# One-hot graph sums on TensorE: four summing matmuls behind each batch of picks, or one after each picked bucket

## The chip, the cores and the metric

The kernel runs on one core of a Trainium2 chip. The metric is device time in microseconds for one execution of the whole program. Three runs of the kernel before are shown, and their median is what a change is measured against. Traces are of one further execution, taken by the hardware profiler. Engines are called as the profile calls them: PE is the matrix engine's matmul, PEld its weight load, DVE the vector engine, ACT the scalar engine, POOL the general one, and SP the one that issues most transfers.

## The reference, cut to what matters

The graph has 6250 nodes with 128 features and 206250 directed edges (100000 drawn pairs in both directions, and a loop at each node). After a layer norm, an encoder and a ReLU, two message layers run, then three averaging layers. The part that the change touches is the message layer:

```python
m = jnp.concatenate([h[row], h[col]], axis=-1)
m = jax.nn.relu(m @ msg_W1[l].T + msg_b1[l])
m = m @ msg_W2[l].T + msg_b2[l]
agg = jax.ops.segment_sum(m, col, num_segments=h.shape[0])
upd = jnp.concatenate([h, agg], axis=-1) @ upd_W[l].T + upd_b[l]
h = _layer_norm(h + upd, ln_g[l], ln_b[l])
```

The first product splits in two: a row of A (source node) plus a row of B (target node) for each edge, then a ReLU. W2 is applied after the sum, since a sum of products is the product of the sum.

## The kernel before, in words

The nodes are cut into 49 blocks of 128. For each target block `w` the edges that end in it are sorted into buckets of up to 128 edges, one bucket for each source block and a 50th for what did not fit. The 50 buckets form 13 batches: twelve of four buckets and a last one of two (`batches`, index `i`). A step is one batch of one target block, and there are 49 x 13 = 637 steps in each of the two message layers (`l`).

**Picks.** `picked` (L556) gets the edges' rows A + B by multiplying with one-hot matrices. Each bucket takes six bfloat16 matmuls of 128x128: three with the source one-hots as weights (L565; A stands in three bfloat16 parts, for accuracy) and three with the target one-hots (L567). So a full step has 24 picks, all into one PSUM bank `pe`, of which there are three. ACT then applies the ReLU into a tile `m` (L574 or L577).

**Sums.** `summed` (L580) adds the rows of a bucket into the target nodes. Its weights are again one-hots, but as 4-byte numbers (`hd`), made by ACT in `widened` (L516). There are two kinds, chosen by `parts`. In the first layer's batches 0, 3, 6, 9 and 12, and in all of the second layer, `m` holds two parts: ACT writes a rounded one (L574), DVE writes what the rounding left (L554, in `refine`), and one float32r matmul of 256 or 258 columns per bucket sums both. In the other batches of the first layer `m` is plain float32 with 129 columns, and each sum shows as two matmul instructions in the trace. These two kinds have the tile names `hd_r` and `hd` in the profile. All sums of a target block go into one PSUM bank `agg`.

**Order.** The code writes one step after the other. A step fetches a later batch's data, makes the one-hots of the batch two ahead (`hot_at`: L88 and L491 on DVE), refines the batch before (`refine`, L554), picks its own batch, widens its own one-hots, and then settles: `settle(2)` sums the batch of two steps ago, since two batches may stay pending. In the second layer four counting matmuls follow (`counts`, L524). Last come single stages of work that lags or leads: the update of the block before (`behind`), the target rows of the next (`other`), and the sort of a later block's edges (`ahead`, first layer only). When the last batch of a block has been summed, `settle` starts that block's update (L590, a copy of `agg` by ACT).

PE executes in the order in which its instructions stand. The framework orders each engine's instructions by the order of the code and by its own plan of when things are ready. On PE the trace has the order that the code writes, while on ACT the casts of L516 run well before the code's place.

Of the kernel before, what the change touches and what calls it, by code (L numbers as in the profile page):

```python
# [67 lines left out]
def fast(tc, dram, ident, miss_i, x, src, dst, weights, columns, rows, out, edges):  # L68
# [12 lines left out]
    with ExitStack() as ctx:  # L81
# [9 lines left out]
        def bank(name="mm"):  # L91
            return psum.tile([B, 512], F32, name=name, bufs={"pe": 3, "so": 1}.get(name, 2))
# [151 lines left out]
        def nodes(w):  # L244
            return slice(w * B, (w + 1) * B)
# [229 lines left out]
        def fetch(l, w, i):  # L475
            cols = batches[i]
            n, c0 = len(cols), cols[0]
            v = both.tile([B, 8, B], BF16, name="v_all", bufs=4)
            nc.sync.dma_start(v[:, :2 * n], svd[w:w + 1, 2 * c0:2 * (c0 + n), :].to_broadcast([B, 2 * n, B]))
            h = None  # L480
            if l == 1:
                h = late.tile([B, 2, B, 2], BF16, name="hd_b", bufs=6)
                nc.sync.dma_start(h[:, :n // 2].rearrange("p r v e -> p (r v e)"), ohd[w, :, c0 * B:(c0 + n) * B])
            spread[l, w, i] = v, h
# [9 lines left out]
        def hot_first(w, i):  # L494

            cols = batches[i]
            n, c0 = len(cols), cols[0]
            hot = early.tile([B, 2, B, 2], BF16, name="hot", bufs=5)
            one_hots(hot[:, :n // 2], sv[w][:, c0:c0 + n])
            t, _ = node_hot(0, w, i)  # L500
            stores.append((ohd[w, :, c0 * B:(c0 + n) * B], hot[:, :n // 2].rearrange("p r v e -> p (r v e)")))
            return t, hot, None

        def hot_again(w, i):

            cols = batches[i]
            n, c0 = len(cols), cols[0]
            t, h = node_hot(1, w, i)
            hs = late.tile([B, 2, B, 2], BF16, name="hs", bufs=4)
            one_hots(hs[:, :n // 2], sources[:, w, c0:c0 + n])  # L510
            return t, h, hs

        def widened(l, i, hot, n):
            hd = (late if l else early).tile([B, 4, B], F32R if parts(l, i) else F32, name="hd_r" if parts(l, i) else "hd",
                                                   bufs=4 if l else 2 if parts(l, i) else 3)
            nc.scalar.copy(hd[:, :n].rearrange("p (r e) v -> p r e v", e=2), hot[:, :n // 2].rearrange("p r v e -> p r e v"))  # L516
            return hd
# [22 lines left out]
        def counted(w, kept):  # L540
            c2 = late.tile([B, B], U8, name="c2")
            nc.vector.tensor_add(c2, kept[0], kept[1])
            stores.append((cnt[w, :, w, :], c2))

        def parts(l, i):

            return l == 1 or i % 3 == 0
# [3 lines left out]
        def refine():  # L551
            while rough:
                m, pe, n = rough.pop(0)
                nc.vector.scalar_tensor_tensor(m[:, :n, :D], pe, 0.0, m[:, :n, D:2 * D].bitcast(F32), op0=OP.max, op1=OP.subtract)  # L554

        def picked(w, l, i, t, b3):  # L556

            cols = batches[i]
            n = len(cols)
            pe = bank("pe")  # L560
            for j, c in enumerate(cols):
                o = slice(j * D, (j + 1) * D)
                block = w if c == NB else c
                for k in range(3):
                    nc.tensor.matmul(pe[:, o], t[:, j, 0, :], a3[l][:, block, k, :], start=(k == 0), stop=False)  # L565
                for k in range(3):
                    nc.tensor.matmul(pe[:, o], t[:, j, 1, :], b3[:, k, :], start=False, stop=(k == 2))  # L567
            pe = pe[:, :n * D].rearrange("p (j f) -> p j f", f=D)
            k = int(parts(l, i))
            ring = rings[k] if l == 0 else late_ring  # L570
            m = ring[turn[k] % len(ring)]
            turn[k] += 1
            if k:
                nc.scalar.activation(m[:, :n, D:2 * D], pe, AF.Relu)  # L574
                rough.append((m, pe, n))
            else:
                nc.scalar.activation(m[:, :n, :D], pe, AF.Relu)  # L577
            return m

        def summed(l, i, m, hd, agg):  # L580

            two = parts(l, i)
            to = agg[:, :2 * D + 2 * (1 - l)] if two else agg[:, D:2 * D + 1]
            for j, c in enumerate(batches[i]):
                nc.tensor.matmul(to, hd[:, j, :], m[:, j, :to.shape[1]], start=(c == 0), stop=(c == NB))  # L585

        def update(w, l, agg):
            xw = xws.pop(w, None)
# [43 lines left out]
        def settle(most):  # L632

            nonlocal behind
            while len(pending) > most:
                w, l, i, m, hd, agg = pending.pop(0)
                if not agg:
                    agg.append(bank("agg"))
                summed(l, i, m, hd, agg[0])
                if i == NI - 1:  # L640
                    for _ in behind:
                        pass
                    behind = update(w, l, agg[0])
                    next(behind)
# [8 lines left out]
        for l in range(2):  # L653
            if l == 1:
                refine()
                settle(0)
                while stores:
                    nc.sync.dma_start(*stores.pop(0))
                part_of.close()
                right.close()  # L660
                h2[0] = ctx.enter_context(tc.tile_pool(name="h2_0", bufs=1, side="right")).tile(
                    [B, NB, 2, D], F32R, name="h2_0")
                late = part_of.enter_context(tc.tile_pool(name="late", bufs=2))
                late_ring = rings[1] + [late.tile([B, 4, 2 * D + 2], F32R, name=f"m2{k}", bufs=1) for k in (2, 3)]
            def fetch_at(q):
                if q < NB * NI:
                    fetch(l, q // NI, q % NI)

            def hot_at(q):
                w, i = divmod(q, NI)  # L670
                if w >= NB:
                    return None
                return hot_again(w, i) if l else hot_first(w, i)

            A = 2
            for q in range(A + 2):
                fetch_at(q)
            hots = [hot_at(q) for q in range(A)]
            kept = []
            for w in range(NB):  # L680
                agg, kept, kept_before = [], [], kept
                b3, b3_next, other = b3_next[0], [], iter(())
                for i, cols in enumerate(batches):
                    q = w * NI + i
                    fetch_at(q + A + 2)
                    while stores:
                        nc.sync.dma_start(*stores.pop(0))
                    hots.append(hot_at(q + A))
                    refine()
                    t, target, source = hots.pop(0)  # L690
                    m = picked(w, l, i, t, b3)
                    hd = widened(l, i, target, len(cols))
                    pending.append((w, l, i, m, hd, agg))
                    settle(2)
                    if l == 1:
                        counts(w, i, source, target, kept)
                        if i == 0 and w:
                            counted(w - 1, kept_before)
                    if i > 1:
                        next(behind, None)  # L700
                        if l == 1:
                            next(behind, None)
                    if i == 4 and (l, w) != (1, NB - 1):
                        other = target_rows((w + 1) % NB, l + (w + 1) // NB, b3_next)
                    next(other, None)

                    for _ in range(2 if steps < q + 2 * NI - 1 and (q < 6 or i % 3 == 0) else 1):
                        next(ahead, None)
                        steps += 1
                    assert i != 6 or l or w + 1 == NB or w + 1 in sv  # L710
                    if l == 1 and i == 6:
                        xws[w] = work.tile([B, D], F32, name="xw")
                        nc.sync.dma_start(xws[w], x[nodes(w), :])
        refine()
        settle(0)
        counted(NB - 1, kept)
        while stores:
            nc.sync.dma_start(*stores.pop(0))
# [296 lines left out]
```

## Time and profile before

| what | value |
|---|---|
| median of three runs | 3890.51 us (3890.47 to 3892.3) |
| the profiled execution's own time | 3893.41 us |
| its span, first to last instruction | 3891.6 us |
| mean granted TensorE clock | 0.996 |
| first message layer, sums on PE | from 102.9 to 1559.8 us |
| second message layer, sums on PE | to 2943.8 us |
| averaging layers | the rest |
| busy in 100 to 1558 us: PE, DVE, ACT | 1452.70, 1364.05, 857.59 us |
| busy in 1558 to 2945 us: PE, DVE, ACT | 1382.28, 1092.70, 1118.35 us |

A line of the timeline has the start in microseconds, the time from the start of the first to the end of the last instruction of the group, the engine, the line of the code, the operation, the tiles written and read, the shapes, and how many instructions are merged. Matmuls overlap one another, so the shown duration of one (219 ns for a pick) is its latency. What a matmul costs PE is the distance from its start to the next one's start.

### The profile page before, as it was taken

The page shows a single profiled execution, that of the slowest core. Times are in us where ns is not written, and L with a number is a line of the kernel's source. Part 1 is how long each engine was busy: PE and PEld are TensorE (multiplying, and loading weights), DVE is VectorE, ACT ScalarE, POOL GpSimd, SP SyncE. Part 2 cuts the span into 40 slices and gives each one's busy share as a digit, 9 for nine tenths or more (in the row PEclk, how much of TensorE's full clock was granted, in tenths as well). Part 3 has the DMA queues.
Part 4 walks back from the last instruction along what each step waited for, and adds up shares of the span by engine and source line. Part 5 has one row for each costly group of instructions (what it writes and reads, how often), then busy time and mean ns, then how long its engine had stood idle before and what let it go on. Part 6 is the DMA issues. An engine that isn't in the chain of part 4 may idle for free. (4 is left out here: it accounts for less than half of the span.)

```text
span 3891.6 us, 117300 instructions
## 1 busy us (share of the span) xinstructions
PE 3820.3 (98%) x45975; PEld 3578.7 (92%) x45975; DVE 2924.2 (75%) x7365; ACT 2531.0 (65%) x4850; POOL 35.1 (1%) x29
## 2 busy tenths in 40 slices
PE   5999999999999999999999999999999999999998
PEld 3999999999999999999999999999998888888887
DVE  7999999999999997787778787877874444444443
ACT  5555555555555555788888888888885555555554
POOL 3000000000000000000000000000000000000000
PEclk8999999999999999999999999999999999999999
DMA  3555555555555555777777777777774444444554
GB/s 107 160 173 167 168 171 175 165 168 172 175 165 168 174 167 169 201 213 211 210 204 214 206 213 212 211 211 206 211 209 136 132 128 114 132 128 114 159 155 124
DMA packets 656079, 671.11 MB, mean 172 GB/s; under 512 B 113200, under 2 KB 504474, under 8 KB 655386
## 3 DMA queue, kind: packets, MB, share of 16 engines
q1 hardware_dynamic: 650124, 662.26, 58.5%
q8 instruction: 362, 5.93, 0.6%
q14 instruction: 203, 1.66, 0.2%
q10 hardware_dynamic: 5390, 1.26, 0.1%
HBM read 534.28 MB, written 128.99 MB: 170 GB/s over the span
## 5 line engine op out<-in xcount | busy, mean ns | idle before, releaser
L565 PE MATMUL pe<-a,ot 128*128 128x128 bf16 x14700 | 1622.0, 219 | 0.0
L567 PE MATMUL pe<-b,ot 128*128 128x128 bf16 x14700 | 1620.7, 219 | 0.0
L565 PEld LDWEIGHTS <-ot 128*128 128x128 bf16 x14700 | 1044.0, 98 | 17.0
L567 PEld LDWEIGHTS <-ot 128*128 128x128 bf16 x14700 | 1026.4, 98 | 0.0
L778 PE MATMUL pe<-cf,h 128*128 128x512 f32 (+1 forms) x3822 | 924.3, 394 | 2.2 <-DVE cf L770 1.1
L778 PEld LDWEIGHTS pe<-cf,h 128*128 128x128 f32 x3822 | 677.3, 190 | 141.9 <-ACT cf L770 1.2
L574 ACT ACTIVATE m<-pe 128x512 fp32r<-128x512 f32 (+1 forms) x882 | 508.2, 576 | 327.3 <-PE pe L567 324.7
L491 DVE TENSOR_SCALAR ot<-v_all,part 128x1024 bf16<-128x1024 bf16 (+1 forms) x1274 | 599.2, 470 | 105.7 <-PE pe L567 87.5
L770 ACT CAST cf<-c 128x2048 fp32r<-128x2048 uint8 (+2 forms) x253 | 433.8, 1714 | 338.7 <-PE pe L778 283.5
L554 DVE SCALAR_TENSOR_TENSOR m<-pe,m 128x512 fp32r<-128x512 f32 (+1 forms) x882 | 579.1, 657 | 56.5 <-ACT m L574 31.0
L585 PE MATMUL agg<-m,hd_r 128*128 128x256 f32 (+1 forms) x3332 | 612.2, 303 | 3.1 <-DVE m L554 3.0
L770 DVE CAST cf<-c 128x2048 fp32r<-128x2048 uint8 (+2 forms) x254 | 280.7, 1105 | 359.0 <-PE pe L778 204.1
L585 PEld LDWEIGHTS agg<-m,hd_r 128*128 128x128 f32 x3332 | 453.9, 190 | 4.0 <-DVE m L554 3.8
L585 PE MATMUL agg<-m,hd 128*128 128x129 f32 x3136 | 435.3, 281 | 0.0
L516 ACT CAST hd_r<-hd_b 128x512 fp32r<-128x512 bf16 (+1 forms) x637 | 384.5, 604 | 8.5 <-DMA hd_b<-ohd 2.6
L585 PEld LDWEIGHTS agg<-m,hd 128*128 128x128 f32 x3136 | 381.0, 191 | 0.0
L516 ACT CAST hd<-hot 128x512 f32<-128x512 bf16 x392 | 242.3, 618 | 194.0 <-DVE hot L88 91.4
L526 ACT CAST ca<-so 128x512 uint8<-128x512 f32 (+1 forms) x637 | 360.2, 565 | 0.4 <-PE so L524 0.4
L577 ACT ACTIVATE m<-pe 128x512 f32<-128x512 f32 x392 | 233.5, 596 | 134.9 <-PE pe L567 133.2
L88 DVE TENSOR_TENSOR hot<-sv,iota 128x512 bf16<-128x512 f16 (+1 forms) x637 | 254.8, 406 | 20.3 <-ACT hd L516 12.0
L88 DVE TENSOR_TENSOR hs<-sources,iota 128x512 bf16<-128x512 f16 (+1 forms) x637 | 258.2, 406 | 5.5 <-PE so L524 1.8
L524 PE MATMUL so<-hd_b,hs 128*128 128x128 bf16 x2450 | 252.2, 222 | 2.3 <-DMA hd_b<-ohd 2.0
(163 smaller groups left out, 3165.2 us busy)
## 6 DMA issues: line engine op xcount, KB each, us to landing
v_all<-svd SPq DMA_DIRECT2D x1176, 256.0 KB, 3.9
c<-cnt SPq DMA_DIRECT2D x216, 512.0 KB, 3.8
ohd<-hot SPq DMA_DIRECT2D x588, 128.0 KB, 3.5
hd_b<-ohd SPq DMA_DIRECT2D x588, 128.0 KB, 3.8
cnt<-ca SPq DMA_DIRECT2D x540, 64.0 KB, 3.6
v_all<-svd SPq DMA_DIRECT2D x98, 128.0 KB, 3.4
xw<-in_x SPq DMA_DIRECT2D x49, 64.0 KB, 3.5
ohd<-hot SPq DMA_DIRECT2D x49, 64.0 KB, 2.2
```

The costliest lines, as they stand in the source:

```text
L88: nc.vector.tensor_tensor(to, v.rearrange("p (r e) -> p r e", e=2).unsqueeze(2).to_broadcast([B, n, B, 2]), iota_2.unsqueeze(1).to_broadca ...
L491: nc.vector.tensor_scalar(t[:, :n].rearrange("p j k s -> p (j k) s"), v[:, :2 * n], part, None, op0=OP.is_equal)
L516: nc.scalar.copy(hd[:, :n].rearrange("p (r e) v -> p r e v", e=2), hot[:, :n // 2].rearrange("p r v e -> p r e v"))
L524: nc.tensor.matmul(pa[:, j * B:(j + 1) * B], source[:, j // 2, :, j % 2], target[:, j // 2, :, j % 2], start=True, stop=True)
L526: nc.scalar.copy(ca[:, :n], pa[:, :n * B].rearrange("p (j d) -> p j d", d=B))
L554: nc.vector.scalar_tensor_tensor(m[:, :n, :D], pe, 0.0, m[:, :n, D:2 * D].bitcast(F32), op0=OP.max, op1=OP.subtract)
L565: nc.tensor.matmul(pe[:, o], t[:, j, 0, :], a3[l][:, block, k, :], start=(k == 0), stop=False)
L567: nc.tensor.matmul(pe[:, o], t[:, j, 1, :], b3[:, k, :], start=False, stop=(k == 2))
L574: nc.scalar.activation(m[:, :n, D:2 * D], pe, AF.Relu)
L585: nc.tensor.matmul(to, hd[:, j, :], m[:, j, :to.shape[1]], start=(c == 0), stop=(c == NB))
L770: (nc.scalar.copy if turn % 2 else nc.vector.tensor_copy)(cf[:, :k, :n].rearrange("p s w d -> p w s d"), c8[:, :n, s % R:s % R + k])
L778: nc.tensor.matmul(p[:, :n * B], h2[l % 2][:, s, k, :], cf[:, s % K, :n].rearrange("p w d -> p (w d)"), start=(s == 0 and k == 0), stop=(s ...
```

## The change

`summed` and `settle` become generators that yield after every sum. `picked` takes such a generator and calls it once after each bucket's six picks. What is left of it is run through behind the picks, before `widened`. Since the pending list now loses its oldest entry before the new one is appended, `settle(2)` becomes `settle(1)`, and the batch summed in a step is the same as before. In a step of four buckets with four sums, PE's order goes from 24 picks and four sums to four times six picks and one sum. A batch of two buckets, each block's last, changes this at its two ends: during its own picks the four sums of batch 10 stand as one sum, six picks, three sums, and its own two sums stand after the first and the second of four buckets.

```diff
-        def picked(w, l, i, t, b3):
+        def picked(w, l, i, t, b3, sums):
...
                 for k in range(3):
                     nc.tensor.matmul(pe[:, o], t[:, j, 1, :], b3[:, k, :], start=False, stop=(k == 2))
+                next(sums, None)
...
             for j, c in enumerate(batches[i]):
                 nc.tensor.matmul(to, hd[:, j, :], m[:, j, :to.shape[1]], start=(c == 0), stop=(c == NB))
+                yield
...
                 if not agg:
                     agg.append(bank("agg"))
-                summed(l, i, m, hd, agg[0])
+                yield from summed(l, i, m, hd, agg[0])
...
                     refine()
                     t, target, source = hots.pop(0)
-                    m = picked(w, l, i, t, b3)
+                    sums = settle(1)
+                    m = picked(w, l, i, t, b3, sums)
+                    for _ in sums:
+                        pass
                     hd = widened(l, i, target, len(cols))
                     pending.append((w, l, i, m, hd, agg))
-                    settle(2)
```

At the end of each layer `settle(0)` is run through in a loop, with the same effect as before.

More of the change, by code (lines that the diff above doesn't have):

```diff
@@ L655, in fast @@
                 refine()
-                settle(0)
+                for _ in settle(0):
+                    pass
                 while stores:
@@ L690, in fast @@
                     t, target, source = hots.pop(0)
-                    m = picked(w, l, i, t, b3)
+                    sums = settle(1)
+                    m = picked(w, l, i, t, b3, sums)
+                    for _ in sums:
+                        pass
                     hd = widened(l, i, target, len(cols))
                     pending.append((w, l, i, m, hd, agg))
-                    settle(2)
                     if l == 1:
@@ L714, in fast @@
         refine()
-        settle(0)
+        for _ in settle(0):
+            pass
         counted(NB - 1, kept)
```

## The prediction

> **What bounds the kernel now.** I read the page's busy times first, then the groups of the sums, then who waits in the two message layers, then single steps in the timeline.
>
> ```profile
> PE 3820.3 (98%) x45975; PEld 3578.7 (92%) x45975; DVE 2924.2 (75%) x7365; ACT 2531.0 (65%) x4850; POOL 35.1 (1%) x29
> L585 PE MATMUL agg<-m,hd_r 128*128 128x256 f32 (+1 forms) x3332 | 612.2, 303 | 3.1 <-DVE m L554 3.0
> L585 PE MATMUL agg<-m,hd 128*128 128x129 f32 x3136 | 435.3, 281 | 0.0
> ```
>
> PE is busy throughout, and busy PE alone proves little, but the last column says that it hardly ever waits ahead of a sum: 3.1 us in 6468 matmuls. Ahead of the picks of L565 and L567 the page has 0.0. PE's order and pitch therefore set the time of both message layers, and there is no idle time on PE that a better order could win back. What remains is what a sum costs by its place. One step each with four and with two sums of the hd_r kind, and one with four of the hd kind (eight matmuls):
>
> ```profile
> 1002.47 0.33 PE L567 MATMUL pe<-b,ot 128*128 128x128 bf16 x3
> 1002.61 0.73 PE L585 MATMUL agg<-m,hd_r 128*128 128x258 f32 x4
> 1003.18 0.34 PE L565 MATMUL pe<-a,ot 128*128 128x128 bf16 x3
> 1003.36 0.33 PE L567 MATMUL pe<-b,ot 128*128 128x128 bf16 x3
> ```
>
> ```profile
> 1000.81 0.33 PE L567 MATMUL pe<-b,ot 128*128 128x128 bf16 x3
> 1000.95 0.49 PE L585 MATMUL agg<-m,hd_r 128*128 128x258 f32 x2
> 1001.28 0.34 PE L565 MATMUL pe<-a,ot 128*128 128x128 bf16 x3
> 1001.46 0.33 PE L567 MATMUL pe<-b,ot 128*128 128x128 bf16 x3
> ```
>
> ```profile
> 1011.65 0.33 PE L567 MATMUL pe<-b,ot 128*128 128x128 bf16 x3
> 1011.82 1.11 PE L585 MATMUL agg<-m,hd 128*128 128x129 f32 x8
> 1012.77 0.33 PE L565 MATMUL pe<-a,ot 128*128 128x128 bf16 x3
> 1012.94 0.33 PE L567 MATMUL pe<-b,ot 128*128 128x128 bf16 x3
> ```
>
> Picks alone come at 0.056 us from start to start (in the rows that follow the first view, 18 of them from 1003.36 to 1004.36), 0.336 a bucket. From the first line to the last of each fence stand six picks and the sums. That leaves 0.89 - 0.336 = 0.554 us for four hd_r sums and 0.65 - 0.336 = 0.314 for two. Two equations: each sum costs 0.120, and a group of sums costs 0.074 on top, whatever its length. The eight hd matmuls leave 1.29 - 0.336 = 0.954.
>
> **Where the fixed cost comes from.** The weight loads around the four sums:
>
> ```profile
> 1002.41 0.21 PEld L567 LDWEIGHTS <-ot 128*128 128x128 bf16 x3
> 1002.58 0.55 PEld L585 LDWEIGHTS agg<-m,hd_r 128*128 128x128 f32 x4
> 1003.17 0.17 PEld L565 LDWEIGHTS <-ot 128*128 128x128 bf16 x3
> ```
>
> Picks' loads follow at 0.056 and the sum's load takes its turn after them (0.17 after the first of three), one matmul ahead at most. Four 4-byte loads span 0.55 where one lasts 190 ns, so they follow at 0.12: in a row each load lies under a sum of about the same length, while the first of a group lies under a 0.056 pick. The pick after the group loads at 1003.17, 0.01 ahead of its matmul and not under the last sum. Both ends are paid once a group.
>
> For the hd kind the same float32 matmul stands in two places, in a row behind others and alone between bfloat16 matmuls:
>
> ```profile
> 1008.37 0.39 PE L254 MATMUL mm<-wt,hT 128*128 128x128 f32 x2
> 1008.59 0.33 PE L565 MATMUL pe<-a,ot 128*128 128x128 bf16 x3
> ```
>
> ```profile
> 2024.21 0.43 PE L254 MATMUL mm<-wt,hT 128*128 128x128 f32 x2
> 2024.49 0.33 PE L565 MATMUL pe<-a,ot 128*128 128x128 bf16 x3
> ```
>
> A pair costs 0.22 to the next pick in the row and 0.28 alone: 0.06 of fixed cost. From the eight: four pairs at 0.22 to 0.225 are 0.88 to 0.90, so 0.954 leaves 0.05 to 0.07. I take 0.055.
>
> **The change, part by part.** It adds and removes no matmul, no DVE or ACT work and no transfer; SP's and POOL's queues keep their order, since fetch and stores stand ahead of the picks as before. What changes is the number of groups.
>
> Extra groups in one target block: first layer, hd_r: batches 0, 3, 6 and 9 go from one group to four (+12), batch 12 from one to two (+1), 13 in all. First layer, hd: batches 1, 2, 4, 5, 7, 8 and 11 +3 each, batch 10, summed in the two-bucket step, +1: 22. Second layer: eleven batches +3, batch 10 +1, batch 12 +1: 35. With 49 blocks: 637 + 1715 = 2352 hd_r groups and 1078 hd groups.
>
> Cost: 2352 x 0.074 = 174.0 us, and 1078 x 0.055 = 59.3 us. All of it is on the path, because PE is what everything waits for. Bounds: the hd_r row at its nearest other is the 0.05 of the hd kind, which makes both kinds 3430 x 0.05 = 171.5; from above 0.08 and 0.065 (the rounding of the rows) make 258. I take 233, since 0.074 is of the same operation in the same place.
>
> The Trainium skill, "TensorE: Matmul & The Clock Gate", speaks against a loss in its section on what each phase is for: the queue pulls weight loads ahead of running matmuls, so that the next weights load while this one multiplies. Taken without limit, that hides every load and the sum is 0, 3890 us. The load rows above show the pull reaching one matmul ahead of a sum, and no further; by them the sum is 233. The same page's section on LDWEIGHTS gives 107 ns for 128 columns as an estimate, which less one pick leaves 51 ns a group and 175 us in all; the row's 0.074 holds the exit as well.
>
> **A wait that comes earlier.** The sums of a batch need DVE's refinement (L554). The first now stands one bucket into the step, three buckets (1.0 us) earlier. Behind it on PE are all later picks, and ACT's ReLU waits for those. In the first layer, at the start of a block:
>
> ```profile
> 1029.69 0.42 DVE L554 SCALAR_TENSOR_TENSOR m<-pe,m 128x256 fp32r<-128x256 f32 x1
> ```
>
> ```profile
> 1030.70 0.48 PE L585 MATMUL agg<-m,hd_r 128*128 128x258 f32 x2
> ```
>
> The refinement ends at 1030.11. That step's picks start at 1029.39, so its first sum would stand at 1029.73, 0.38 too early. In the next step the refinement ends at 1031.62 and the first sum would stand at 1031.37, 0.25 too early. That is 0.63 x 49 = 31 us if DVE stands where it stood. But a block gets 13 x 0.074 + 22 x 0.055 = 2.2 us longer on PE, with DVE's work unchanged, so DVE comes earlier by more than it lacks. I take 0, and 31 as the end. In the second layer DVE waits 42 times, 102.9 us in all, for the transfer of xw (L619). After one such wait the refinement ends at 2038.60, and the sums at 2039.27 would stand 1.0 earlier, at 2038.26: 0.34 too early, 42 x 0.34 = 14 us at most. Transfers don't get slower, steps get longer: I take 7. A gain is excluded here, since PE has only those 3 us to win. DVE's waits for picks (L491, 87.5 us) move with PE and cost nothing, being DVE's idle time.
>
> **Sum.** 174 + 59 + 7 = 240 us. Against the profiled execution's own 3893.4 us this is 4133; that execution stands 2.9 us above the median of the runs, so against the median 3890.5 + 240 = 4130.
>
> **Rivals.**
> - *A lone group is cheaper* (0.05 for both kinds, no stall): 171.5, so 4062. For it: the hd kind shows 0.05 to 0.06. Against it: four and two hd_r sums agree on 0.074.
> - *Refinement stalls PE* as often as today's places say: 233 + 31 + 14 = 278, so 4169. For it: DVE is 94% busy in the first layer (1364 of 1458 us). Against it: the longer block.
> - *The loads hide after all* (the other side). If a sum's load could start two matmuls ahead, entry and exit vanish; an hd_r sum would cost what its columns take, under 0.115 (256 columns at 0.056 for 128 are 0.112), and the 2450 hd_r sums would gain at least 0.008 each, 20 us, and today's 882 groups their 0.074, 65 us: 3805. It decides as soon as a lone sum costs less than the present mean of 0.554 / 4 = 0.139. Against it: the load of 1002.58.
> - *The order stays*: the framework's plan sets each engine's order, on ACT it moves casts (L516) ahead. If sums are not ready in its plan they bunch behind the picks again: 3890. Against it: on PE every group stands where the code writes it.
>
> **How the numbers follow.** My forecast 0.75 (4100 to 4150), cheaper groups 0.09, stalls 0.08, order stays 0.04, loads hidden 0.03, other 0.01. The range takes in the cheaper groups and the stalls together with the upper price (258 + 45 = 303 us): 4055 to 4190. 0.2% of this time is 7.8 us, about what a measurement can tell from no change. Faster 0.04, same 0.03, slower 0.93.
>
> **What the profile after would show.** A lone hd_r sum between picks takes 0.19 (0.120 + 0.074) beyond the picks, a lone hd pair 0.28; loads of L585 still start right after a pick's; in a row of four steps PE shows x1 and x2 groups of L585 in place of x4 and x8. Idle time ahead of L585 stays under 10 us in all. The first layer grows by about 106 us (47 + 59) and the second by about 134 (127 + 7). The prediction is wrong if lone sums cost 0.14 or less, if PE's order is not the code's, or if L585 waits for L554 tens of microseconds.

## The result, and the profile after

The changed kernel takes 4112.78 us (median of four runs) against 3891.41 us before (four runs): a ratio of 1.057, 95% interval 1.0555 to 1.0586. It is 221 us slower. The granted clock was 0.995, against 0.996 in the profile before. The forecast was 240 us slower, 4130 us, with a range of 4055 to 4190.

The profile after, first the page's line of busy times and the groups of the sums (L586 is L585 of before, one line further down), then the largest of PE's waits in the two message layers:

```profile
PE 4044.9 (98%) x45975; PEld 3704.2 (90%) x45975; DVE 2944.7 (72%) x7365; ACT 2481.2 (60%) x4850; POOL 35.1 (1%) x29
L586 PE MATMUL agg<-m,hd_r 128*128 128x256 f32 (+1 forms) x3332 | 1184.1, 360 | 2.1 <-DVE m L554 1.9
L586 PE MATMUL agg<-m,hd 128*128 128x129 f32 x3136 | 669.1, 300 | 0.0
```

```profile
engine line waited for: us in total, times, longest us
PE agg L586 <- DVE m L554: 1.9, 3, 0.9
```

The same matmuls in the same number, PE at 98% as before, and still next to no waiting: 1.9 us ahead of the sums (3.0 before). The 221 us are spent inside PE's stream. The two groups' busy times grew from 612 to 1184 and from 435 to 669 us, but that is only the union of latencies, since four sums in a row overlap one another and lone ones don't. What counts is the distance between starts. Here are two lone sums and the picks around them, from PE's timeline of the changed kernel at the place where a batch of the hd kind (two matmuls a sum) gives way to one of hd_r:

```profile
1075.59 0.33 PE L567 MATMUL pe<-b,ot 128*128 128x128 bf16 x3
1075.76 0.44 PE L586 MATMUL agg<-m,hd 128*128 128x129 f32 x2
1076.04 0.33 PE L565 MATMUL pe<-a,ot 128*128 128x128 bf16 x3
1076.20 0.33 PE L567 MATMUL pe<-b,ot 128*128 128x128 bf16 x3
1076.34 0.36 PE L586 MATMUL agg<-m,hd_r 128*128 128x258 f32 x1
1076.55 0.34 PE L565 MATMUL pe<-a,ot 128*128 128x128 bf16 x3
1076.72 0.33 PE L567 MATMUL pe<-b,ot 128*128 128x128 bf16 x3
```

From 1075.59 to 1076.20 are six picks (0.336) and one hd sum: 0.61 - 0.336 = 0.274 us for the sum. From 1076.20 to 1076.72 it is 0.52 - 0.336 = 0.184 us for one hd_r sum. Measured over all such places by the starts of the matmuls, the medians are 0.277 and 0.188. In a row of four they cost 0.947 / 4 = 0.237 and 0.552 / 4 = 0.138. So a sum between picks costs 0.04 to 0.05 us more than one in a row, and an added group costs 0.188 - 0.120 = 0.068 (hd_r) or 0.277 - 2 x 0.112 = 0.053 (hd).

The loads of the same place, on PEld, from the second load of that hd sum on:

```profile
1075.81 0.19 PEld L586 LDWEIGHTS agg<-m,hd 128*128 128x128 f32 x1
1075.92 0.27 PEld L565 LDWEIGHTS <-ot 128*128 128x128 bf16 x3
1076.15 0.21 PEld L567 LDWEIGHTS <-ot 128*128 128x128 bf16 x3
1076.32 0.19 PEld L586 LDWEIGHTS agg<-m,hd_r 128*128 128x128 f32 x1
1076.54 0.17 PEld L565 LDWEIGHTS <-ot 128*128 128x128 bf16 x3
```

The hd_r sum's load comes 0.17 after the first of three picks' loads, in its turn and no earlier, and the next pick's load comes 0.22 later, 0.01 ahead of its matmul at 1076.55. What the row of four paid once is now paid at every sum.

By the starts, the time is lost behind the first matmul of a group. In a lone hd pair the second load begins 0.110 us after the first, as 4-byte loads do in a row, but the matmul ahead started only 0.054 after its own load. So this second load comes 0.056 us after that matmul's start (1075.81 after 1075.76), where the next loads of a row come 0.002 after, and the second matmul stands at 0.166 in place of 0.112 us (medians of all such pairs). The 0.054 between these two is the fixed cost of the hd kind. Behind a lone hd_r sum the next pick's load begins 0.202 us after the sum's start, and the pick 0.004 later.

The two layers can be taken apart by the starts of their matmuls: the first runs from the first pick to the last hd sum, the second from there to the last hd_r sum.

| kernel | first layer, us | second layer, us |
|---|---|---|
| before | 1461.1 | 1384.0 |
| after | 1560.4 (+99.2) | 1502.9 (+118.9) |
| added groups, 637 x 0.068 + 1078 x 0.053 | +100.5 | |
| added groups, 1715 x 0.068 | | +116.6 |

The count of groups times the cost of one gives each layer to within 3 us.

### The profile page after: what moved, and what is told of

The parts are those of the page before. It is cut to its first block, busy times and chain, and to the rows that moved or that the text cites. A ratio compares the mean times of both kernels' runs of the same rounds, so it can differ in the third digit from the quotient of the medians.

```text
span 4111.6 us, 117158 instructions
## 1 busy us (share of the span) xinstructions
PE 4044.9 (98%) x45975; PEld 3704.2 (90%) x45975; DVE 2944.7 (72%) x7365; ACT 2481.2 (60%) x4850; POOL 35.1 (1%) x29
## 3 DMA queue, kind: packets, MB, share of 16 engines
q1 hardware_dynamic: 650124, 662.26, 54.4%
## 5 line engine op out<-in xcount | busy, mean ns | idle before, releaser
L565 PE MATMUL pe<-a,ot 128*128 128x128 bf16 x14700 | 1648.1, 221 | 0.0
L586 PE MATMUL agg<-m,hd_r 128*128 128x256 f32 (+1 forms) x3332 | 1184.1, 360 | 2.1 <-DVE m L554 1.9
L565 PEld LDWEIGHTS <-ot 128*128 128x128 bf16 x14700 | 996.7, 98 | 120.0
L567 PEld LDWEIGHTS <-ot 128*128 128x128 bf16 x14700 | 1026.6, 98 | 0.0
L586 PE MATMUL agg<-m,hd 128*128 128x129 f32 x3136 | 669.1, 300 | 0.0
L776 ACT CAST cf<-c 128x2048 fp32r<-128x2048 uint8 (+2 forms) x253 | 433.8, 1715 | 339.4 <-PE pe L784 278.1
L586 PEld LDWEIGHTS agg<-m,hd_r 128*128 128x128 f32 x3332 | 625.3, 190 | 3.7 <-DVE m L554 3.5
L586 PEld LDWEIGHTS agg<-m,hd 128*128 128x128 f32 x3136 | 465.5, 191 | 0.0
L524 PE MATMUL so<-hd_b,hs 128*128 128x128 bf16 x2450 | 252.2, 222 | 1.9 <-DMA hd_b<-ohd 1.6
```

The costliest lines, as they stand in the source:

```text
L524: nc.tensor.matmul(pa[:, j * B:(j + 1) * B], source[:, j // 2, :, j % 2], target[:, j // 2, :, j % 2], start=True, stop=True)
L776: (nc.scalar.copy if turn % 2 else nc.vector.tensor_copy)(cf[:, :k, :n].rearrange("p s w d -> p w s d"), c8[:, :n, s % R:s % R + k])
```

## The experiments

Two theories stood against each other. One is that of the prediction: a group of 4-byte sums has a fixed cost, because its first weight load is longer than the pick that should cover it. The other is that the place matters: sums among picks switch the PSUM bank, break the run of picks, or need their refinement earlier. Every ratio is to the kernel before as timed in the same round; its medians there were 3890.64 us (e1, e2, e4, e5), 3892.04 (e3, e6) and 3894.16 (e7, e8).

**Two sums after each of the first two buckets (e1_pairs).**

```diff
                 nc.tensor.matmul(to, hd[:, j, :], m[:, j, :to.shape[1]], start=(c == 0), stop=(c == NB))
-                yield
+                if j % 2:
+                    yield
```

> Two sums stand after the first bucket and two after the second, so a full step has two groups of sums (four in the changed kernel, one before); everything else is as in the changed kernel. Theory (a fixed cost for each group of sums, 0.068 us of the hd_r kind and 0.052 of the hd kind, as the lone sums of the changed kernel show): extra groups over before are 16 x 49 = 784 of hd_r and 8 x 49 = 392 of hd, so 53 + 20 = 74 us, 3965 us. Rival (the cost comes from sums standing among the picks at all, or from the earlier need of the refinement, not from the number of groups): the first sum stands where it stands in the changed kernel, so most of the 221 us stays, 4060 or more.

Measured: 3985.06 us against 3890.64, ratio 1.0242 (1.0223 to 1.026), 94 us slower where 74 were expected and the rival asked for 170 or more. Two groups in the place of four give less than half of the loss. PE's timeline shows the pair at its expected price:

```profile
2000.37 0.33 PE L567 MATMUL pe<-b,ot 128*128 128x128 bf16 x3
2000.51 0.48 PE L586 MATMUL agg<-m,hd_r 128*128 128x256 f32 x2
2000.83 0.34 PE L565 MATMUL pe<-a,ot 128*128 128x128 bf16 x3
2001.01 0.33 PE L567 MATMUL pe<-b,ot 128*128 128x128 bf16 x3
```

0.64 - 0.336 = 0.304 us a pair; the median of all is 0.307 to 0.309, and two such pairs less one row of four are 0.06 to 0.07. The expectation left out two things. PE's waits for the refinement rose from 3.0 to 8.8 us, in the loads' own view from 3.8 to 13.6. And at two places a block a float32 matmul of the update (in the lines of before: L249, and L602, L603 and L254 together) had stood right behind a row of sums and shared its load time; behind picks it pays 0.05 itself, 5 us in all. Together that is 11 to 15 of the 20 us; the rest was not traced.

**Sums in a row, ahead of the picks (e2_front).**

```diff
+                    settle(1)
                     m = picked(w, l, i, t, b3)
...
-                    settle(2)
```

> All four sums of a batch stand in a row ahead of the step's picks instead of behind them: as many groups as before, but a whole step's picks (1.34 us) earlier. Theory of groups alone: 3891 us, less up to 15 us because in the second layer the update's float32 matmuls now join a group of sums. Theory of the prediction about the early wait: steps get no longer here, so DVE has no time to catch up, and the refinement (L554) would come late by 0.38 + 0.34 and 0.25 + 0.34 us at two steps of each of 49 blocks in the first layer (64 us) and by 0.68 us after each of 42 waits for xw in the second (28 us): 3940 to 3980, with idle time ahead of L585 of tens of us. Rival (position costs more than grouping): well above 4000.

Measured: 3989.19 us, ratio 1.0261 (1.0243 to 1.028), 99 us slower with no group added. The loads' waits name the cause:

```profile
PEld agg L585 <- DVE m L554: 102.3, 140, 2.4
```

102 us of waiting in 140 places, for the refinement alone. The layers took 1530.8 and 1410.2 us, 69.7 and 26.2 more than before. By the starts of the matmuls the long waits sum to about 70 us in the first layer and 45 in the second, where the update's matmuls that now join a group give some of it back. The estimates of 64 and 28 were low, the second by more. So an early need of the refinement can cost 100 us here, and it was not this that the changed kernel paid: its row says 1.9. There the first sum stands only one bucket later than here, but the blocks are longer; this run alone doesn't part the two.

**Two-part sums in bfloat16, in the order of before (e4_bf16_row) and in that of the changed kernel (e5_bf16_lone).** The same edit on both kernels:

```diff
-                 [both.tile([B, 4, 2 * D + 2], F32R, name=f"m2{k}", bufs=1) for k in range(2)]]
+                 [both.tile([B, 4, 2 * D + 2], BF16, name=f"m2{k}", bufs=1) for k in range(2)]]
...
-            hd = (late if l else early).tile([B, 4, B], F32R if parts(l, i) else F32, name="hd_r" if parts(l, i) else "hd",
+            hd = (late if l else early).tile([B, 4, B], BF16 if parts(l, i) else F32, name="hd_r" if parts(l, i) else "hd",
...
-                late_ring = rings[1] + [late.tile([B, 4, 2 * D + 2], F32R, name=f"m2{k}", bufs=1) for k in (2, 3)]
+                late_ring = rings[1] + [late.tile([B, 4, 2 * D + 2], BF16, name=f"m2{k}", bufs=1) for k in (2, 3)]
```

> The order of before. The two-part batches hold their parts and the one-hots that sum them in bfloat16 in place of float32r, so these sums lose some accuracy; the plain float32 batches of the first layer are as before. Theory (a 4-byte weight load of some 0.11 us that a pick of 0.056 us can't cover): a bfloat16 load lasts no longer than a pick, so the fixed cost of these groups goes and each sum costs its 256 columns, 0.112 us by the pitch of the picks. A group of four goes from 0.552 to 0.448, one of two from 0.312 to 0.224: 784 x 0.104 + 98 x 0.088 = 90 us less, 3801 us. Rival (the cost lies in switching the PSUM bank or in leaving the run of picks): each sum 0.112 but the fixed 0.07 stays, 882 x 0.07 = 62 us less gain, 3863.

> The order of the changed kernel with the bfloat16 sums of the run before it. Theory (weight loads): lone sums of the two-part batches cost no more than in a row, and only the 1078 extra groups of plain float32 sums cost 0.052 us each: 56 us over the bfloat16 kernel with sums in a row, 3857. Rival (switching banks or order): the 2352 extra groups cost their 0.068 us still, 216 us over the row.

Measured: 3815.74 us in a row, ratio 0.9806 (0.9788 to 0.9824), and 3902.47 us alone, ratio 1.0034 (1.0018 to 1.0049). The row gained 75 us, where 90 were expected and the rival asked for 28. A group of four shrank by the expected 0.104, but by starts PE's waits for the refinement grew from some 4 to 16 us. The timelines of PE, four in a row and one lone sum, in the two kernels:

```profile
1902.58 0.33 PE L567 MATMUL pe<-b,ot 128*128 128x128 bf16 x3
1902.75 0.60 PE L585 MATMUL agg<-m,hd_r 128*128 128x256 bf16 x4
1903.19 0.39 PE L524 MATMUL so<-hd_b,hs 128*128 128x128 bf16 x4
```

```profile
1900.97 0.33 PE L567 MATMUL pe<-b,ot 128*128 128x128 bf16 x3
1901.14 0.27 PE L586 MATMUL agg<-m,hd_r 128*128 128x256 bf16 x1
1901.25 0.33 PE L565 MATMUL pe<-a,ot 128*128 128x128 bf16 x3
```

The loads around that lone sum:

```profile
1900.92 0.21 PEld L567 LDWEIGHTS <-ot 128*128 128x128 bf16 x3
1901.09 0.10 PEld L586 LDWEIGHTS <-hd_r 128*128 128x128 bf16 x1
1901.14 0.26 PEld L565 LDWEIGHTS <-ot 128*128 128x128 bf16 x3
```

Four in a row take 0.44 us from their start to the next matmul's, one alone takes 0.11. A lone bfloat16 sum has no fixed cost at all, though it stands at the same place among the picks and switches between the same PSUM banks as the float32r sum that cost 0.188. That refutes the rival of place and bank, and shows that the cost belongs to the 4-byte operands. The load rows point at the load: the bfloat16 one takes 98 ns where the 4-byte one takes 190, and the next pick's load begins 0.002 us after the sum's start (1901.14 both), where it came 0.202 after a lone float32r sum. The edit changed the weights and the rows of `m` together, though, so it doesn't part a long load from 4-byte data. For the hd kind the starts of the loads above do; for hd_r it stays open whether the load or the matmul holds the next load back.

But the two kernels are 87 us apart, not 56. The first layer gives 54.4 (1439.5 to 1493.9 us), as its 1078 float32 groups should. The second gives 29.5 (1332.7 to 1362.2) where 0 was expected, and PE waits again:

```profile
PE agg L586 <- DVE m L554: 43.1, 47, 2.8
```

```profile
DVE xw L621 <- DMA xw<-in_x: 99.5, 40, 3.6
```

Of these 47 waits 43 lie in the second layer (39.9 us), one in nearly every block. In one of them DVE's timeline has, in order, the addition to xw held 3.15 us by its transfer, and the refinement behind it; PE's has the sum that waits for it:

```profile
1667.85 0.29 DVE L621 TENSOR_TENSOR xw<-xw,row 128x128 f32<-128x128 f32 x1 [3.15 <-DMA xw<-in_x]
...
1668.99 0.68 DVE L554 SCALAR_TENSOR_TENSOR m<-pe,m 128x512 bf16<-128x512 f32 x1
```

```profile
1669.73 0.27 PE L586 MATMUL agg<-m,hd_r 128*128 128x256 bf16 x1 [1.37 <-DVE m L554]
```

**Eight in a row, in every second step (e3_eight, and with bfloat16 e6_bf16_eight).**

```diff
-                    settle(2)
+                    if q % 2:
+                        settle(2)
```

> Sums only in every second step, those of two batches in a row (eight, behind 48 picks): half as many groups of sums as before. Theory (a fixed cost for each group): in the second layer 318 groups fewer at 0.068 us, in the first 318 fewer at about 0.055 us, so 39 us less, with 3 us given back where float32 matmuls of the update lose their neighbours: 3855 us, faster than before. Rival (four in a row is simply the place where sums do least harm, and the loss of the changed kernel has to do with position): no gain, 3890 or slower because refinement and one-hots must be held longer.

> Eight in a row as in the run before, with the two-part batches' sums in bfloat16 (some accuracy less). Theory: bfloat16 groups have no fixed cost to save, and only some 98 pairs of neighbouring float32 batches merge, 5 us: 3811 us, the same as the bfloat16 kernel with four in a row (3816). Rival (eight in a row helps for another reason, such as the refinement being needed later): again some 30 us or more below 3816.

Measured: 3871.01 us against 3892.04, ratio 0.9948 (0.9931 to 0.9964), and with bfloat16 3826.97, ratio 0.9837 (0.982 to 0.9853). The first gains 21 us of the 36 expected; the second loses 11 against four in a row in place of gaining 5. The groups themselves behave: eight hd_r sums cost 1.02 us at the median where two rows of four cost 2 x 0.55, so 0.07 to 0.08 is saved, and sixteen hd matmuls 1.841 for 2 x 0.947, so 0.053.

```profile
2004.28 0.33 PE L567 MATMUL pe<-b,ot 128*128 128x128 bf16 x3
2004.42 1.19 PE L585 MATMUL agg<-m,hd_r 128*128 128x256 f32 x8
2005.45 0.41 PE L524 MATMUL so<-hd_b,hs 128*128 128x128 bf16 x4
```

Some 15 us are given back elsewhere in both kernels: the counting matmuls wait for their loads, the transposition of the finished sums waits for DVE (L597, 8.6 us on PEld in the bfloat16 kernel), and float32 matmuls of the update pay their own load. These were not costed one by one.

**The wait behind the 30 us (e7_lone_late_xw, e8_row_late_xw).** The two additions into xw swap places, on both bfloat16 kernels. The one that needs only the transfer then stands behind one that needs a matmul of the update, and can't be drawn ahead:

```diff
-            nc.vector.tensor_add(xw, xw, row[:, R_OUT, :])
             yield
             nc.vector.tensor_add(xw, xw, p[:, :D])
+            nc.vector.tensor_add(xw, xw, row[:, R_OUT, :])
```

> The lone bfloat16 sums once more, with one thing changed in the update: the two additions into xw swap places, so the one that needs only the transferred xw (L621 there) can't be drawn ahead on DVE and held there by the transfer. Theory (that wait delays the refinement, and PE stands for it): in the second layer 45 waits ahead of lone sums took 49.9 us and go, less some 3 us that stay, so 3902 falls to about 3855, and the distance to the bfloat16 row is what the 1078 extra float32 groups cost, 56 us, less what the row gains by the same swap. Rival (the refinement is late because DVE has too much to do, or for another reason): 3900 as before.

> The bfloat16 sums four in a row, with the same swap in the update. Theory: of PE's waits ahead of these sums 13.5 us lie in the second layer, most of it beyond the usual 0.03 to 0.06 us each; some 10 us go, 3806 us. Rival: the swap lengthens the update's chain and brings nothing, 3816.

Measured: 3856.41 us alone, ratio 0.9904 (0.9887 to 0.992), and 3811.32 in a row, ratio 0.9791 (0.9774 to 0.9807). The lone sums win back 46 us (50 with each run set against its own round's kernel before) of the 47 expected, and PE's wait of 43.1 us is now this:

```profile
PE agg L586 <- DVE m L554: 3.1, 4, 1.3
```

The second layer then takes 1317.1 us with lone sums and 1321.9 in a row: without 4-byte sums and without that wait, lone sums cost nothing. The row gained 4 us by the swap (8 against its own round) where 10 were expected, and the intervals of its two ratios overlap, so the gain in time isn't shown, though PE's wait for the refinement fell from 9.2 to 0.7 us. In the first layer, where the float32 sums remain, lone sums cost 1493.6 - 1437.6 = 56.0 us, and 1078 x 0.052 is 56.1. The bfloat16 sums in a row, with the late addition, are faster than both kernels, by 2.1% against the one before. Two bfloat16 parts hold fewer bits of the messages than two float32r parts do.

## Why the prediction was right

**PE's order sets the time.** Right. Every engine has as many instructions as before, and PE waits as little.

**The fixed cost of a group.** Right in kind, a little high in size: 0.074 for hd_r came from two lengths of row, and a lone sum shows 0.068; 0.055 for hd measured 0.053. On 2352 and 1078 groups that is 14 and 2 us too much, and the 7 for the wait makes 23; the forecast was only 19 too high, since the whole kernel lost 4 us more than its groups explain. The prediction says that four and two sums "agree on 0.074", but two rows give two unknowns and test neither; the lone sum did. Half of the 0.006 is the rounding of the rows: the medians, 0.551 and 0.311, give 0.071. The rest comes from the straight line, since the second sum of a row adds 0.123 and the later ones 0.120.

**The count of groups.** Right: by layer, the count times the measured cost gives 100.5 and 116.6 us for the measured 99.2 and 118.9. The forecast had 106 and 134.

**Where the cost comes from.** The prediction read it out of the load rows, as the load sticking out from under a pick. For the hd kind the starts of the loads in the changed kernel show just that. For hd_r the bfloat16 pair ties the cost to the 4-byte operands: without them it is 0.00 at the same place. The Trainium skill, "TensorE: Matmul & The Clock Gate", section on weight-path perf modes, says that the fast weight load is on for 128 weights of any type but FP32, about twice as fast; the bfloat16 runs agree in size (98 against 190 ns for a load, 0.108 against 0.188 us for a lone sum). Its statement that loads are pulled ahead of running matmuls holds here for one load ahead: in the traces before and after, no pick's or sum's load begins before the matmul ahead of its own has started.

**The wait that comes earlier.** The 0 for the first layer was right, the 7 for the second too much: 1.9 us in all. Its price of 14 us "at most" came from one wait (2037.32 on DVE, which the profile puts down to another transfer, cnt). It was no bound: in e2_front, where twice that was expected in the second layer, the waits were 45. The reason given, that longer steps let DVE and the transfer of xw catch up, fits every run, though no run changes the step's length alone: where steps got no longer (e2_front) PE waited some 100 us, where the second layer's steps got shorter (e5_bf16_lone) 43, and with the transfer's wait off DVE's path 3.

**The rivals.** The cheaper group (0.05 for both kinds) fell for hd_r; the stalls did not come; the loads didn't hide; and PE's order was the code's. Two sums on record are slightly off without bearing on this: there are 3332 hd_r sums, not 2450, which are those of the second layer alone, so the loads that hide would have given 3799 in place of 3805; and the highest price of 303 us makes 4194, just over the range's 4190.

## What to carry to other kernels

Before splitting a row of matmuls, read the distance between starts for two lengths of the row: the intercept is what each new group will cost. In these traces a 4-byte load, which the next follows at 0.11 to 0.12 us, was covered by a sum of that length ahead of it and not by a pick of 0.056, so such matmuls belong in a row. Holding both operands of the two-part sums in bfloat16, at some loss of accuracy, was worth more than a longer row: 75 us, where eight in a row in place of four gave 21. Whether bfloat16 weights alone would do, as one-hots are exact in it, wasn't tried. An order that moves a consumer forward brought next to no waiting here where it also made the period longer (the changed kernel) or where the producer's engine was no longer held by a transfer (e7_lone_late_xw). In e5_bf16_lone and e2_front, which had neither, PE waited 43 and some 100 us. When the same order is tried on a faster kernel, its waits have to be read again.

## What was not expected

- The two kinds end differently. After a float32r sum the next bfloat16 load doesn't start under the running matmul: at the end of a row it comes 0.119 us after the last sum's start (the median before L565; 0.117 before L524). After a plain float32 matmul it comes 0.002 us after (both in the kernel before). The prediction saw this late load in one row of hd_r and took it for a cost paid at the end. Little is paid there: the pick behind a row starts 0.123 us after the last sum, about the pitch in the row, and the three picks from there take some 0.01 us more. That is most of 0.068 against 0.053; whether it is the whole difference wasn't tried.
- An addition that takes DVE 0.29 us held it 2.45 us on average in 42 of 49 blocks in the kernel before, since it was drawn ahead of a transfer that had not landed. In the order of before PE waited 3 us for the refinement in all; with lone bfloat16 sums, swapping two additions won 46.
